# A four-layer graph network on one core: two chunks of the last layer by fetched neighbour lists, and two reorderings in the first layers

## The chip, the cores and the metric

The kernel runs on one core of a Trainium2 chip. The metric is the device time of one execution in microseconds (us). A profile of one execution shows what each engine did: TensorE (PE; its weight loads are PEld), VectorE (DVE), ScalarE (ACT), GpSimd (POOL), SyncE (SP), and the 16 DMA engines that move data.

## The reference

There are 2708 nodes with 512 features in `x`, and `adj` is a symmetric matrix of zeros and ones in which a node has about 16 neighbours. Four layers follow one another. Each adds its result to its input and normalizes every row.

```python
deg = jnp.maximum((adj != 0).astype(jnp.float32).sum(-1), 1.0)
x = _layernorm(x + _L0_gnn_ref(x, adj, deg[..., None], L0_gnn_W, L0_gnn_b), axis=-1)
x = _layernorm(x + _L1_gnn_ref(x, adj, L1_gnn_W, L1_gnn_b), axis=-1)
x = _layernorm(x + _L2_gnn_ref(x, adj, L2_gnn_W_stack), axis=-1)
x = _layernorm(x + _L3_gnn_ref(x, adj, L3_gnn_W, L3_gnn_b), axis=-1)
```

Layer 0 is `relu(((D (adj + I) D) x + x) W + b)` with `D = rsqrt(deg)`. Layer 1 is `(D' adj D' x) W^T + b`, where `D'` comes from the row sums of `adj`. Layer 2 is twice an attention: scores of every pair of nodes, a softmax over all nodes, multiplied by `adj`, and a weighted sum of the rows. Layer 3 is `adj (x W) + b`, with the eight heads side by side.

## The kernel before

**Tiling.** The nodes are 22 blocks of 128 (the last, block 21, has 20). `CH` cuts the result columns into six chunks: four of 512, then 384 and 276. `GROUPS` cuts the 22 blocks that are summed over into six groups: four of 4 blocks, then two of 3. Layers 0, 1 and 3 compute, for each chunk `k`, the transposed sum `acc[d] = sum over blocks j of x_j[:, d]^T adj[j, chunk]` in four banks (`d` is a quarter of the features). `multiply` does one group of one chunk. Each product is made twice, with the high part of the rows (`xh`) and the low part (`xl`), which `halve` makes in the first chunk. The factor from `adj` is a page `m`, which `prepare` casts on ScalarE from bytes (`at`) loaded by `load_bytes`; layer 0 casts from floats and writes the bytes (`masks`) for the layers after. `evict` copies `acc` to pages `ht`, `project` multiplies these by the weights (`mm`), and `combine` and `finish` add the residual (`xres`), normalize and store.

**Order.** Every engine runs its instructions in the order in which the program issues them (`Ordered`). `step` is one group: `before_products` loads two groups ahead and prepares one ahead, then come the products, then one phase of `ends` of the chunk before. Pages (82 of them, 128 by 512 floats) and banks come from pools: a new tile waits until the last use of the tile that had its place has ended, DMAs included.

**Layer 0.** The last group of a chunk is followed by `degree_ends`: products with ones count the neighbours (`deg`, `cnt`), VectorE makes `dg` of them, POOL multiplies four pages `xt` by `dg`, VectorE works out `dis` and `rdeg`, and then `evict` adds `xt` to `acc` as it writes `ht`.

**Layer 1.** `prepare` ends with `note`: VectorE takes maxima over the bytes in pieces of 32 nodes (`feeds`). From them `index` makes, later and between other work, the lists `givers`: for each block the numbers of the rows that are neighbours of its nodes. A full block has 4 lists of 128 rows that serve all its nodes and 8 that serve one quarter each; block 21 has 3.

**Layer 2.** `Attention` computes in the same chunks. `scores` fills pages `s`, `soften` takes the exponent, sums (`sum`), multiplies by the bytes and stores to `pairs` in HBM, beside three copies of the value rows (`pairs<-z_sb`). `fetch` gathers the rows of a list with an indirect DMA on POOL (`g`), into 11 wide buffers, and `weigh` makes `acc<-g`; lists of quarters go four side by side. A clock of planned costs (`advance`, `later`) decides where in the order of issue these stand. `normalize` ends a chunk of the second attention: the rows `r` are stored to `saved[2]` by SP (`x<-r`).

**Layer 3.** The first three chunks (`TWO = 3`) multiply their groups 0 to 3 while the attention ends (`early`). After that `step` goes through groups 4 and 5 of chunks 0 to 2 and all groups of chunks 3 to 5. Residual rows come through POOL's queue (`residual`).

Of the kernel before, what the change touches and what calls it, by code (L numbers as in the profile page):

```python
# [8 lines left out]
FP = mybir.dt.float32  # L9
# [10 lines left out]
P = 128  # L20
N = 2708
# [21 lines left out]
PAGES, WIDES = 82, 11  # L43
TWO = 3
LN_EPS = 1e-5
DEG_EPS = 1e-8
# [41 lines left out]
class Kernel:  # L88


    def __init__(self, ctx, tc, x_in, x_t, adj, adj_t, w0, b0, w1, b1, w2, w2_t, w3, b3, out):
# [33 lines left out]
            scratch.tile([P, D], FP, tag=f"y_{i}", name=f"y_{i}") for i in range(NB)  # L125
        ]

        self.masks = [
# [357 lines left out]


def cost(columns):

    return 4 * columns / 2400  # L490
# [25 lines left out]
class Fast:  # L516
# [4 lines left out]
    def __init__(self, kernel):  # L521
        self.k, self.tc = kernel, kernel.tc
        self.nc = Ordered(kernel.tc)

    def page(self, name, dtype=FP, shape=(P, BANK)):
# [8 lines left out]
    def run(self):  # L534
        kernel, nc = self.k, self.nc
        with ExitStack() as ctx:
# [10 lines left out]
            self.attention = attention = Attention(self)  # L547
            self.jobs, self.due, self.other, self.beats = [], None, 1, 0
            run = Run(l0, l1)
            for t in range(len(run.seq)):  # L550
# [11 lines left out]
            run.seq += [(l3, k, g) for k in range(2, TWO) for g in (4, 5)]  # L562
            run.seq += [(l3, k, g) for k in range(TWO, len(CH)) for g in range(len(GROUPS))]
            attention.run(self.early(run))
            for j in range(*GROUPS[5]):
                l3.rows[j] = attention.made[j]
            for t in range(4 * TWO, len(run.seq)):
                self.step(run, t)

            ly, k = run.before  # L570
# [236 lines left out]
    def prepare(self, ly, k, g, between=None, late=False):  # L807


        nc, (c0, cw) = self.nc, CH[k]  # L810
        ats = ly.done.pop(("at", k, g), None)
        if ats is None:
            return
        ms = []
        for j, at in zip(range(*GROUPS[g]), ats):
            if k == 0:
                self.halve(ly, j)
            m = self.page(f"m{ly.number}_{k}_{j}", FR)
            nc.scalar.copy(m[:, :cw], at[:, :cw])
            ms.append(m)  # L820
            if between:
                between()
                between = None
        ly.done["m", k, g] = ms
        if ly.number == 0:
            self.examining = self.examine(ly, k, g, ats)
            if k == 0 or g > 0:
                self.checked()
            else:
                next(self.examining)  # L830
        if ly.number == 1:
            at = ly.done.pop(("bytes", k, g))
            if late:
                return lambda: self.note(k, g, at)
            self.note(k, g, at)

    def note(self, k, g, at):
# [55 lines left out]
    def multiply(self, ly, k, g, only=None, ds=range(DC)):  # L893
# [9 lines left out]
        if blocks[-1] == NB - 1:  # L903


            blocks = blocks[:-1]
            for x in (ly.hi, ly.lo):
                for d in range(DC):
# [28 lines left out]
    def degree_ends(self, ly, k):  # L937
# [22 lines left out]
        for c in range(DC):  # L960
            nc.gpsimd.tensor_mul(xt[c][:, :cw], xt[c][:, :cw], dg[:, :cw])
        for _ in self.rsqrt(self.k.dis[:, i0 : i0 + n], cnt, DEG_EPS):
            pass
# [49 lines left out]
    def residual(self, ly, k):  # L1013
        for i, _, _ in blocks_of(k):
            t = self.page(f"xres{ly.number}_{i}")
            self.nc.gpsimd.dma_start(t, ly.source[i])
            ly.done["xres", i] = t
# [64 lines left out]
    def before_products(self, run, t):  # L1082
# [23 lines left out]
        if t + 1 < len(seq) and seq[t + 1][0].number == ly.number:  # L1106
            self.prepare(*seq[t + 1])
        if ly.number == 0 and g == len(GROUPS) - 2:
# [5 lines left out]
    def step(self, run, t):  # L1114
# [6 lines left out]
        if ly.number == 1 and k == len(CH) - 1 and g in (2, 3, 4):  # L1121
            self.attention.begin(g - 2)
        self.multiply(ly, k, g)
        if g == len(GROUPS) - 1 and k in ly.begun:
# [4 lines left out]
        if run.before:  # L1129
            self.ends(run, run.phase)  # L1130
            run.phase += 1
            if run.phase in ((3, 4, 5) if wide else (4,)):
                self.work("DVE")
        if g == (4 if ly.number == 3 and k < TWO else 3):
            self.residual(ly, k)
        if g == len(GROUPS) - 1:
            if ly.number == 3:
                self.biased(ly, k)
            if ly.number == 0:
                ends = self.degree_ends(ly, k)  # L1140
                next(ends)
                if k == len(CH) - 1:
                    note = self.prepare(
                        *run.seq[t + 1], between=lambda: next(ends), late=True
                    )
                for _ in ends:
                    pass
            while run.before and run.phase < 2:
                self.ends(run, run.phase)
                run.phase += 1  # L1150
            if k in ly.acc:
                self.evict(ly, k)
            if ly.number == 0:
                self.checked()
            run.before, run.phase = (ly, k), 0
# [212 lines left out]
class Attention:  # L1368
# [29 lines left out]
    def blank(self):  # L1398
# [3 lines left out]
        for pairs in (p for ly in self.pairs for p in ly):  # L1402
            self.nc.sync.dma_start(
                pairs[N:, : 2 * PAIR + D].rearrange("j (r d) -> j r d", d=D),
                t[:n, :].unsqueeze(1).to_broadcast([n, (2 * PAIR + D) // D, D]),
            )

    def begin(self, step):
# [370 lines left out]
    def normalize(self, ch):  # L1779
# [4 lines left out]
        def rest():  # L1784
            for _ in work:
                pass
            for (i, _, _), (r, _) in zip(ch.blocks, ch.ends):
                self.nc.sync.dma_start(self.k.saved[2][i], r)
                self.made[i] = r

# [113 lines left out]


@with_exitstack
def kernel(
# [61 lines left out]
```

## Time and profile before

| | us |
|---|---|
| median of 3 runs | 2306.28 |
| lowest, highest | 2305.75, 2307.77 |
| the profiled execution, whole | 2307.16 |
| its span, first to last instruction | 2305.3 |
| TensorE busy in the span | 2272.8 |
| VectorE, ScalarE, POOL busy | 1409.5, 675.9, 706.5 |
| bytes moved | 486.34 MB, 211 GB/s on average |
| mean granted TensorE clock | 0.995 |

A line of the profile's groups reads: line, engine, operation, output <- input, shapes, count; then busy time and the mean of one in ns; then the idle time of the engine just before, and what ended it. A line of the timeline reads: start, length, engine, line, operation, tiles, and in brackets the idle time before it with its releaser. Almost every line of code is L71 because a helper issues all instructions, so groups are told apart by their tiles. Products are pipelined, and their ends are modelled: the distance between two starts says more than a length. Of layer 3, chunk 3's projection begins at 2214.03 us and chunk 5's products end at about 2284.4.

### The profile page before, as it was taken

The page shows a single profiled execution, that of the slowest core. Times are in us where ns is not written, and L with a number is a line of the kernel's source. Part 1 is how long each engine was busy: PE and PEld are TensorE (multiplying, and loading weights), DVE is VectorE, ACT ScalarE, POOL GpSimd, SP SyncE. Part 2 cuts the span into 40 slices and gives each one's busy share as a digit, 9 for nine tenths or more (in the row PEclk, how much of TensorE's full clock was granted, in tenths as well). Part 3 has the DMA queues.
Part 4 walks back from the last instruction along what each step waited for, and adds up shares of the span by engine and source line. Part 5 has one row for each costly group of instructions (what it writes and reads, how often), then busy time and mean ns, then how long its engine had stood idle before and what let it go on. Part 6 is the DMA issues. An engine that isn't in the chain of part 4 may idle for free.

```text
span 2305.3 us, 25891 instructions
## 1 busy us (share of the span) xinstructions
PE 2272.8 (99%) x8525; PEld 1292.4 (56%) x8525; DVE 1409.5 (61%) x2803; ACT 675.9 (29%) x1354; POOL 706.5 (31%) x822
## 2 busy tenths in 40 slices
PE   9999999999999999999999999999999999899997
PEld 6676777778644444443555444444443455476685
DVE  6777886786554538748667511228769789625523
ACT  7444352323111123222332200113222334342211
POOL 3333431111000001635466550001635467542000
PEclk9999999999999999999999999999999999999999
DMA  9966762222556505868699998504868799973311
GB/s 347 288 189 179 188 182 76 76 82 77 194 191 263 182 5 181 296 205 300 236 331 336 337 411 320 185 5 165 301 228 288 250 324 332 338 219 120 117 51 43
DMA packets 260929, 486.34 MB, mean 211 GB/s; under 512 B 40238, under 2 KB 126950, under 8 KB 260784
## 3 DMA queue, kind: packets, MB, share of 16 engines
q1 hardware_dynamic: 192128, 269.63, 33.6%
q0 software_dynamic: 68656, 214.96, 28.0%
q8 instruction: 69, 1.13, 0.2%
q14 instruction: 76, 0.62, 0.1%
HBM read 307.55 MB, written 176.92 MB: 210 GB/s over the span
## 4 chain that ended last, share of the span: by engine, by line
PE 87%; DMA 5%; DVE 4%; issue 2%; ACT 1%; POOL 1%; SPq 0%; DVEq 0%; POOLq 0%; ACTq 0%
PE sp L71 33%; PE acc L71 30%; PE mm L71 8%; PE z L71 6%; PE wst L71 6%; DMA at<-in_adj_t 1%; DMA g<-pairs,givers 1%; PE mix L71 1%; DMA xr<-y 1%; PE list L71 1%; DMA mask<-some 1%; DMA x<-x 0%; PE tr_x2t L71 0%; PE tr_x2b L71 0%; DVE xl L71 0%
## 5 line engine op out<-in xcount | busy, mean ns | idle before, releaser
L71 PE MATMUL sp<-xs,wst_sb 128*128 128x512 f32 (+3 forms) x2112 | 798.3, 545 | 0.0
L71 POOL DMA_INDIRECT g<-pairs,givers x510 | 525.6, 1031 | 870.6 <-DMA xr<-x 242.3
L71 PEld LDWEIGHTS sp<-xs,wst_sb 128*128 128x128 f32 (+1 forms) x2112 | 380.5, 186 | 407.7 <-issue 325.6
L71 PE MATMUL acc<-m,xh 128*128 128x512 f32 (+4 forms) x1584 | 567.8, 380 | 7.4 <-ACT m L71 5.8
L71 PE MATMUL acc<-m,xl 128*128 128x512 f32 (+4 forms) x1584 | 551.0, 366 | 3.5 <-DVE xl L71 3.5
L71 PEld LDWEIGHTS acc<-m,xh 128*128 128x128 f32 (+1 forms) x1584 | 288.6, 188 | 72.0 <-issue 21.6
L71 PEld LDWEIGHTS acc<-m,xl 128*128 128x128 f32 (+1 forms) x1584 | 289.1, 189 | 48.0 <-issue 5.5
L71 PE MATMUL acc<-g 128*32 128x512 f32 (+1 forms) x1020 | 265.7, 609 | 2.9 <-DMA g<-pairs,givers 2.5
L71 ACT COPY s<-sp 128x512 f32<-128x512 f32 (+2 forms) x252 | 132.6, 528 | 396.3 <-PE sp L71 389.8
L71 ACT ACTIVATE s<-s 128x512 f32<-128x512 f32 (+3 forms) x264 | 151.7, 580 | 323.5 <-DVE s L71 323.2
L71 DVE TENSOR_TENSOR top<-top,s 128x512 f32<-128x512 f32 (+2 forms) x240 | 149.4, 623 | 155.6 <-ACT s L71 153.9
L71 PE MATMUL mm<-w,ht 128*128 128x512 f32 (+1 forms) x528 | 224.1, 594 | 3.4 <-DVE ht L71 3.4
L71 ACT CAST m<-at 128x512 fp32r<-128x512 uint8 (+5 forms) x396 | 199.6, 567 | 60.9 <-DMA at<-mask 20.2
L71 DVE TENSOR_TENSOR s<-s,shift 128x512 f32<-128x512 f32 (+3 forms) x264 | 162.9, 620 | 38.2 <-ACT shift L71 38.2
L71 DVE TENSOR_TENSOR s<-s,a 128x512 f32<-128x512 f32 (+3 forms) x264 | 165.9, 628 | 15.1 <-DMA a<-mask 6.0
L71 DVE TENSOR_TENSOR sum<-sum,s 128x512 f32<-128x512 f32 (+4 forms) x252 | 156.9, 623 | 13.9 <-ACT s L71 13.9
L71 PEld LDWEIGHTS mm<-w,ht 128*128 128x128 f32 (+1 forms) x528 | 95.9, 186 | 121.2 <-issue 111.4
L71 PEld LDWEIGHTS acc<-g 128*32 128x32 f32 (+1 forms) x1020 | 75.8, 135 | 146.1 <-issue 118.0
L71 PE MATMUL z<-w,xt 128*128 128x512 f32 (+1 forms) x352 | 151.0, 596 | 0.0
L71 PE MATMUL wst<-xt,mixed 128*128 128x512 f32 (+2 forms) x384 | 150.5, 545 | 0.0
L71 POOL DMA_DIRECT2D x<-o x44 | 26.0, 597 | 354.8 <-DVE o L71 350.6
L71 PEld LDWEIGHTS wst<-xt,mixed 128*128 128x128 f32 x384 | 72.1, 190 | 71.0 <-issue 59.0
(168 smaller groups left out, 1495.3 us busy)
## 6 DMA issues: line engine op xcount, KB each, us to landing
pairs<-z_sb SPq DMA_DIRECT2D x84, 768.0 KB
pairs<-s SPq DMA_DIRECT2D x168, 256.0 KB
at<-in_adj_t SPq DMA_DIRECT2D x84, 256.0 KB
xres<-x POOLq DMA_DIRECT2D x44, 256.0 KB, 4.9
x<-o POOLq DMA_DIRECT2D x43, 256.0 KB, 2.9
pairs<-s SPq DMA_DIRECT2D x84, 128.0 KB
x<-x SPq DMA_DIRECT2D x37, 256.0 KB
at<-mask SPq DMA_DIRECT2D x32, 256.0 KB
```

The lines of the kernel that those rows point to most:

```text
L71: ins = call(*args, **kw)
```

## The change

Two parts of layer 0 and 1, and one of layer 3 with what feeds it.

- **Layer 3.** The products run over chunks 0 to 3 only. Blocks 16 to 21 (chunks 4 and 5) are computed by a new class `Listed`: it gathers the rows of each list from a new tensor `sided`, sums them with products like those of the attention, turns the sum with four transposes, projects it and finishes it. A row of `sided` holds, for each pair of blocks, 128 columns of `adj`, the 512 features of the row, and 128 columns of `adj`. Its gathers begin after the attention; its products stand between those of chunk 3 from group 1 on, by a planned clock.
- **What feeds it.** `give` stores the cast pages `m` of layer 1's last two chunks to `sided` as floats (88 stores on SP). `normalize` stores each block of rows three times to `sided`, on SP, behind the store to `saved[2]` of the same block. `blank` writes zeros to the rows past the last node. `residual` of layer 3 uses SP's queue.
- **Layer 0.** In the last group of a chunk the products of `d` 0 and 1 come first, then the counting products, then `d` 2 and 3. `degree_ends` yields after POOL's products, and its last part comes behind `evict`.
- **Layer 1.** In chunk 0, `note` of groups 1 to 5 is put off: one is done in group 2, two each in groups 3 and 4, what is left at the end.

```diff
+DENSE = 4
+LISTED = CH[DENSE][0] // P
+SIDED = D + 2 * P
...
-            run.seq += [(l3, k, g) for k in range(TWO, len(CH)) for g in range(len(GROUPS))]
+            run.seq += [(l3, k, g) for k in range(TWO, DENSE) for g in range(len(GROUPS))]
...
+            self.listed = Listed(self, l3)
             for t in range(4 * TWO, len(run.seq)):
                 self.step(run, t)
+            self.listed.end_all()
...
+            if ly.number == 1 and k >= DENSE:
+                self.give(k, j, m)
...
+    def give(self, k, j, m):
+        n, lo, cw = rows_of(j), 0, CH[k][1]
+        while lo < cw:
+            i = (CH[k][0] + lo) // P - LISTED
+            w = min(P if i % 2 == 0 else 2 * P, cw - lo)
+            at = i // 2 * SIDED + i % 2 * (D + P)
+            self.nc.sync.dma_start(
+                self.k.sided[j * P : j * P + n, at : at + w], m.bitcast(FP)[:n, lo : lo + w]
+            )
+            lo += w
...
-            for x in (ly.hi, ly.lo):
+            for x in (ly.hi, ly.lo) if 0 in ds else ():
...
             nc.gpsimd.tensor_mul(xt[c][:, :cw], xt[c][:, :cw], dg[:, :cw])
+        yield True
...
-            self.nc.gpsimd.dma_start(t, ly.source[i])
+            (self.nc.sync if ly.number == 3 else self.nc.gpsimd).dma_start(t, ly.source[i])
...
-            self.prepare(*seq[t + 1])
+            late = ly.number == 1 and (k, g) < (0, len(GROUPS) - 1)
+            note = self.prepare(*seq[t + 1], late=late)
+            if late:
+                self.notes.append(note)
...
-        self.multiply(ly, k, g)
+        if self.listed and k == DENSE - 1 and g > 0:
+            for d in range(DC):
+                self.multiply(ly, k, g, ds=[d])
+                self.listed.beside(few_us(k, g) / DC)
+        elif ly.number == 0 and g == len(GROUPS) - 1:
+            self.multiply(ly, k, g, ds=range(2))
+            ends = self.degree_ends(ly, k)
+            next(ends)
+            self.multiply(ly, k, g, ds=range(2, DC))
+        else:
+            self.multiply(ly, k, g)
+            if self.listed:
+                self.listed.advance(few_us(k, g))
...
+        if ly.number == 1 and k == 0:
+            for _ in range(max(0, g - 1) if g < len(GROUPS) - 1 else len(self.notes)):
+                if self.notes:
+                    self.notes.pop(0)()
...
             if ly.number == 0:
-                ends = self.degree_ends(ly, k)
-                next(ends)
                 if k == len(CH) - 1:
...
-                for _ in ends:
-                    pass
+                else:
+                    next(ends)
+                next(ends)
...
             if ly.number == 0:
+                for _ in ends:
+                    pass
                 self.checked()
...
                 self.nc.sync.dma_start(self.k.saved[2][i], r)
+                rows = self.k.sided[i * P : (i + 1) * P, P:]
+                self.nc.sync.dma_start(
+                    bass.AP(
+                        rows.tensor,
+                        rows.offset,
+                        [rows.ap[0], (SIDED, (NB - LISTED) // 2), (1, D)],
+                    ),
+                    r.unsqueeze(1).to_broadcast([P, (NB - LISTED) // 2, D]),
+                )
...
+class Listed:
+    AHEAD = WIDES - 1
...
+    def beside(self, us):
+        self.advance(us)
+        end = self.clock + 1.6 * us
+        while self.clock < end and self.weigh():
+            pass
...
+    def weigh(self, wait=False):
+        nc, f = self.nc, self.f
+        if not self.to_weigh:
+            return False
+        i, n, ts, first, last = self.to_weigh[0]
+        there = self.fetched[len(ts) - 1][1]
+        if there > self.clock:
+            if not wait:
+                return False
+            self.advance(there - self.clock)
+        self.to_weigh.pop(0)
+        gs = [self.fetched.pop(0)[0] for _ in ts]
+        if first:
+            self.acc = f.bank(self.half, f"acc3_{i}")
+        odd, side = (i - LISTED) % 2, len(ts) > 1
+        for h, g in enumerate(gs):
+            lo, rows = (h * QW, QW) if side else (0, n)
+            e, z = (D + lo, 0) if odd else (0, P - lo)
+            nc.tensor.matmul(
+                self.acc[lo : lo + rows],
+                g[:, e : e + rows],
+                g[:, z : z + D],
+                start=first,
+                stop=last,
+            )
+        self.advance(1.1 if side else cost(D))
+        if last:
+            acc = self.acc
+            self.later(0, lambda: self.turn(i, n, acc))
+        self.fetch_ahead()
+        return True
...
+    def end_all(self):
+        while self.to_weigh or self.pending:
+            if not self.weigh(True):
+                self.advance(self.pending[0][0] - self.clock)
```

`Listed.fetch_ahead` keeps ten gathers ahead and plans 1.3 us for each and 6 us to land. `turn` copies the sum with VectorE, transposes it, copies it back with ScalarE and adds the bias to the residual rows; `project` makes `mm`; `end` adds, takes the statistics, and after every second block normalizes and stores.

## The prediction

> **What bounds the kernel now.** I read the page first, then the waits of TensorE, then the chain in order of time for layer 3, and then the stage in which layer 2 ends.
>
> ```profile
> PE 2272.8 (99%) x8525; PEld 1292.4 (56%) x8525; DVE 1409.5 (61%) x2803; ACT 675.9 (29%) x1354; POOL 706.5 (31%) x822
> PE 87%; DMA 5%; DVE 4%; issue 2%; ACT 1%; POOL 1%; SPq 0%; DVEq 0%; POOLq 0%; ACTq 0%
> ```
>
> TensorE is busy for 2272.8 of 2305.3 us and makes 87% of the chain that ended last: time is saved by taking work from TensorE or by closing its few gaps. The timeline of TensorE, with each gap and its releaser in brackets, shows those that the change can touch:
>
> ```profile
> 66.30 14.00 PE L71 MATMUL mm<-w,ht 128*128 128x512 f32 x32 [0.72 <-DVE ht L71]
> 227.10 13.14 PE L71 MATMUL mm<-w,ht 128*128 128x512 f32 x30 [1.25 <-DVE ht L71]
> 271.28 9.28 PE L71 MATMUL mm<-w,ht 128*128 128x512 f32 x21 [1.44 <-DVE ht L71]
> 331.57 0.49 PE L71 MATMUL acc<-m,xh 128*128 128x512 f32 x1 [1.07 <-ACT m L71]
> 333.60 0.79 PE L71 MATMUL acc<-m,xl 128*128 128x512 f32 x1 [1.53 <-DVE xl L71]
> 2004.71 0.50 PE L71 MATMUL acc<-m,xh 128*128 128x512 f32 x1 [3.42 <-ACT m L71]
> 2016.20 0.50 PE L71 MATMUL acc<-m,xh 128*128 128x512 f32 x1 [1.60 <-ACT begun L71]
> ```
>
> Three belong to layer 0 (ht), two to layer 1's first chunk, two to the end of layer 2. From 2016 us to the end of the products nothing holds TensorE. Layer 3's end in the chain (start, length, what):
>
> ```profile
> 2214.03 13.73 PE mm L71 x32
> 2227.76 28.38 PE acc L71 x176
> 2256.14 10.30 PE mm L71 x24
> 2266.44 18.06 PE acc L71 x143
> ```
>
> The acc pieces hold 144 of chunk 4's 176 products and all of chunk 5's; mm is a projection. The same chain around 1990:
>
> ```profile
> 1988.11 5.12 DMA x<-r
> ...
> 1993.32 0.56 DVE sum L71
> ...
> 2009.22 4.30 DMA pairs<-s
> ...
> 2016.20 44.96 PE acc L71 x200
> ```
>
> and the windows of 10 us there (length; busy PE, PEld, DVE, ACT, POOL; clock; DMA share; GB/s):
>
> ```profile
> 1980.00:1990.00 10.00, 9.95 (x28) 4.56 (x28) 7.19 (x17) 1.25 (x2) 7.83 (x8) 0.91 0.99 375
> 1990.00:2000.00 10.00, 10.00 (x45) 8.26 (x44) 7.85 (x20) 4.46 (x8) 2.86 (x3) 1.00 1.02 374
> ```
>
> Here TensorE is not the bound. Four rows r of attention chunk 3 are stored (x<-r, issued at 1987.17); VectorE's sum copy cannot start until the store has landed, since its page is one that r held; it heads the softening of chunk 5, whose last stores gate ScalarE's casts and so TensorE at 2016.20. And the DMA engines are full: share 1.0, 374 GB/s.
>
> **What the Trainium skill says.** "DMA: Bandwidth & Descriptors", section "Issuing engines are not separate DMA queues": DMAs of all issuing engines run on the same 16 DMA engines and interleave. The trace agrees: the 1 MB of x<-r takes 6.1 us to land (1987.2 to 1993.3) beside POOL's gathers. Its section "Queues, rings and completion order": each engine takes turns between the queues that have work, packet by packet; so SP's stores and POOL's gathers should share the bandwidth about equally. No row shows the turns themselves. "TensorE: Matmul & The Clock Gate", section "What's actually happening": after an idle window of about 3.4 us TensorE runs at half clock until busy again for as long. The trace has it after less: the gaps at 331 and 333 us are followed by six products 0.43 us apart instead of 0.227.
>
> **Layer 3, removed.** Chunk 4 and 5's products: 28.38 + 18.06 from the chain, and chunk 4's first group, which lies in the piece before, 32 x 0.173 (spacing of the 384-wide products in the timeline) = 5.5: 52.0 us. Their projections: 10.30 + 8.7 (2284.4 to 2293.1) = 19.0.
>
> **Layer 3, added.** Five full blocks, each 4 lists alone and 2 rounds of 4 quarters side by side, and block 21 with 3 lists. A list is the attention's acc<-g product: 3.43 us for four in the chain's pieces, so 0.858; a round of quarters takes 1.06 in the timeline. 23 x 0.858 + 10 x 1.06 = 30.3. Each block's sum is turned by four transposes (tr_top: 0.49 to 0.60 us): 6 x 0.5 = 3.0. Projections 5 x 3.43 + 1.0 = 18.2. Sum of removed and added: -71.0 + 51.5 = -19.5 us on TensorE.
>
> **Are the lists there in time?** There are 63 gathers, each 0.95 us on POOL plus 0.30 between them (the POOL timeline: 1.26 us pitch), landing 4.0 to 4.8 us after issue where DMA is calm. Ten go out at once behind the end of attention; some 77 us of layer 3's other products cover them. The other 53 start as buffers come free in chunk 3: 53 x 1.26 = 67 us, against 75 us of TensorE work there as I add it up in the order of the clock that Listed keeps. POOL is not continuous, for only ten are in flight: following the order with these prices, the last gather goes out about 152 us after group 4 of chunk 0 begins (2099), and TensorE wants it at 155; it lands at 156 to 157. So 1.6 us of wait, then about 1.0 for the last block's copy on VectorE before its transposes and 0.9 for ScalarE's before its projection: nothing is ordered between them. With half a microsecond of colder clock: +4. Ends: +2 if gathers land in 3.5, +10 if their pitch is 1.5. In (3, 1) VectorE has chunk 2's combine and finish (about 7 us) ahead of block 16's copy: some 2 us of wait, which the gathers would otherwise have cost, so not added. After the last projection the tail (12.1 us from the last mm to the end) has the same operations: chunk 3's last block instead of chunk 5's. Layer 3: -15.5.
>
> xres loads go from POOL to SP. Ahead of at<-mask on SP stands out<-o today, till 2135.8, and POOL's xres of those steps went out by 2132; nothing is later. 0.
>
> **Layer 0 and 1.** The count's products go ahead of half of the last group, so POOL's four xt products (5.06 us) and ht come 1 to 1.8 us sooner, and rsqrt's steps go behind ht. The three gaps sum to 3.4; I take 2.5 (0 to 3.4; a both not yet ready could cost 1 of it). In layer 1 two feeds maxima of 2.2 us leave VectorE's queue ahead of the late xl: 4.4 against gaps of 2.6, plus 1.3 of half clock; I take 3 (1 to 3.9). Later they fill idle VectorE time (it is 64% to 87% busy there). Sum -5.5. The 88 small stores of layer 1's casts (give) are about 0.37 us each on SP (the median of pairs<-z_sb): 8 per group, 3 us in steps of 4 to 5.5 us, and the byte loads behind them are two groups ahead; DMA is at 0.23. 0, or +2 if a cast waits. Four stores of zeros near 73 us: 0, at most +1 at the existing gap of 97 us.
>
> **The moved traffic: 22 stores of rows into sided.** Each writes a row block three times, as pairs<-z_sb does: 768 KB. They stand in SP's queue between the x<-r of a chunk, 3.1 MB for four blocks, 17 MB in all. Where chunk 3 ends (1987) the engines are full, r's pages now come free only when these too have landed, and the chain runs through that. SP then has 4.2 MB; about 2.9 MB of gathers share with it (six more issued, about three outstanding): 7.1 MB at 400 GB/s is 17.7 us, and about 1 to land: 2006 instead of 1993.3. That is 12; which page sum gets is not certain (the third r would be 2 us sooner), so 11, all of it on TensorE, which stands from 2001 on. Behind the stores in SP's queue are the row loads x<-x and softening's pairs<-s; those are wanted later than sum's page. Bounds: 0 to 14; nothing there is made faster. The bursts at 1700 and 1799 delay a<-mask by 8 us or so, while the first masked product comes 24 us after the load (1703 to 1727); at 1896 the s pages come back later, with four banks of 2 us to cover; at 2055 and 2101 DMA is at 0.5 to 0.8 and one cast already waits 2.1 us for x<-r with 3.8 us in hand. For all of these +2 (0 to 12).
>
> **Sum.** -15.5 - 5.5 + 11 + 2 = -8. The profiled execution took 2307.16 around its span of 2305.3 and is 0.9 above the median 2306.28; from the median, 2298.3, and I write 2299.
>
> **Rivals.** (1) The burst stays hidden: the page that sum waits for is another, or the stores land ahead of the gathers. For it: many pages, a choice I cannot see. Against it: sum, a cast and an xl all wait for x<-r there. -15.5 - 5.5 + 2: 2287. (2) Slower: the stores hold up softening at every chunk's end, at 1700, 1799 and 1896, through pages of s or masks that come back 8 to 12 us late, ScalarE's copies stop, and TensorE's score banks fill. Against: bank cover, and no ScalarE wait of this kind now beyond 1.5 us. It decides from 12.6 us in sum, about 4 us for each end; with 6 each, 18 in the place of the 2 counted, it is 2314. (3) The gathers set layer 3's end: pitch 1.5 instead of 1.26 puts TensorE 8 us later: 2306, no change. Against: gaps in DMA there (0.2 to 0.3).
>
> **Numbers.** 0.2% of the median is 4.6 us, about what a measurement of this kernel tells from nothing. The likeliest case 0.50 (own range 2292 to 2306), rival (1) 0.25, (2) 0.14, (3) 0.11. Faster: 0.43 of the first and all of (1), 0.68; same: 0.06 of the first, most of (3) and a little of (2), 0.18; slower 0.14. Range: 2286 to 2309.
>
> **What the changed profile would show.** Right: no acc products of 384 or 276 columns in layer 3, gathers into sided's lists at 1.26 us, a copy and two gaps of about 1 us before the last projection; the ht gaps of layer 0 and the xl gap at 333 gone; and, near 2000, a TensorE gap of some 15 us behind ScalarE's casts, with a DMA of sided in the chain in the place of x<-r. Wrong: that gap as it was (rival 1), or new waits of sp products in 1700 to 1930 (rival 2), or acc<-g waits summing to over 8 us after 2180 (rival 3).

## The result: 0.5% slower

The changed kernel takes 2318.85 us (median of 6 runs, 2315.47 to 2319.65), the kernel before 2306.02 beside it: a ratio of 1.005 with a 95% interval of 1.0038 to 1.0061, 12.8 us slower. The prediction said 2299 and at most 2309. The profiled execution took 2319.55 us around a span of 2317.8.

TensorE does have less to do, as the page after says (busy time of each engine, then the chain by engine):

```profile
PE 2260.6 (98%) x8323; PEld 1254.4 (54%) x8323; DVE 1395.0 (60%) x2812; ACT 659.7 (28%) x1313; POOL 757.0 (33%) x863
PE 87%; DMA 6%; DVE 4%; ACT 2%; issue 1%; SPq 1%; POOL 0%; ACTq 0%; DVEq 0%; POOLq 0%
```

It is busy 12.2 us less in a span 12.5 us longer, so it stands still some 25 us longer (products at a slow clock count as busy). To see where, I set the same TensorE instructions of both traces beside each other (start in us; `begun` are pages in which ScalarE keeps the sums that layer 3's early products have begun):

| instruction | before | after | after minus before | lost since the row above |
|---|---|---|---|---|
| first turn of layer 1's rows (tr_x2t) | 388.0 | 387.8 | -0.2 | -0.2 |
| first wst (layer 1 is over) | 604.8 | 614.4 | +9.7 | +9.8 |
| last sp (last scores of layer 2) | 1948.0 | 1958.6 | +10.7 | +1.0 |
| acc restart behind begun (layer 3 runs freely) | 2016.2 | 2033.3 | +17.1 | +6.5 |
| last mm (last projection) | 2292.5 | 2300.8 | +8.2 | -8.9 |
| end of span | 2305.3 | 2317.8 | +12.5 | +4.3 |

Only one stretch is clearly faster, layer 3, and by less than said. The timeline of TensorE after, with the gaps that answer to those shown of before:

```profile
97.26 0.50 PE L76 MATMUL acc<-m,xh 128*128 128x512 f32 x1 [3.26 <-ACT m L76]
100.02 0.80 PE L76 MATMUL acc<-m,xh 128*128 128x512 f32 x1 [2.02 <-ACT m L76]
609.68 0.60 PE L76 MATMUL acc<-m,xh 32*128 32x276 f32 x4 [8.06 <-ACT m L76]
2021.84 0.79 PE L76 MATMUL acc<-m,xh 128*128 128x512 f32 x1 [5.68 <-ACT m L76]
2033.33 0.50 PE L76 MATMUL acc<-m,xh 128*128 128x512 f32 x1 [1.48 <-ACT begun L76]
2280.27 1.11 PE L76 MATMUL tr<-ident,sum 128*128 128x128 f32 x4 [4.05 <-DVE sum L76]
2282.06 5.55 PE L76 MATMUL mm<-w,turned 128*128 128x512 f32 x8 [0.68 <-ACT turned L76]
```

The three ht gaps of layer 0 and the two of layer 1 at 331 and 333 us are gone, as the reorderings intended. But the gap near 97 us, 1.0 before, is now 5.3 in two pieces; one of 8.1 has come at 609 us, where nothing stood before; and two stand at the very end. Three of these are ScalarE's casts being late; the last is VectorE's queue. The chain after, at layer 3's end:

```profile
2270.94 3.45 PE mm L76 x8
2274.41 0.70 DVE xres L76
...
2276.04 2.38 DVE xres L76 x4
2278.43 1.20 DVE ht L76 x2
2280.27 1.13 PE tr L76 x4
2282.06 15.87 PE mm L76 x32
```

Between the last list and its transposes VectorE first ends block 19 (it waits for its mm until 2274.41), then adds the biases of chunk 3's four blocks and copies two ht. All of that was put into its queue ahead of the copy of the last list's sum.

At 609 us one must go two engines back. The timeline of SP's queue after:

```profile
589.65 3.75 SPq L76 DMA_DIRECT2D sided<-m  x8
...
600.62 0.40 SPq L76 DMA_DIRECT2D at<-mask  x1
```

and of ScalarE:

```profile
608.56 1.07 ACT L76 CAST m<-at 128x276 fp32r<-128x276 uint8 x3 [12.48 <-DMA at<-mask]
```

The eight stores of give could not go out before 589.65, since the casts they read stood on ScalarE behind a copy (sums<-list) that waited for TensorE until 589.03. Behind them in SP's queue stand eight weight loads and then the last load of mask bytes; in the kernel before, SP issued that load 18 us earlier:

```profile
582.76 0.32 SPq L71 DMA_DIRECT2D at<-mask  x1
```

It went out late, and the last casts with it.

Finally, each gap costs more than its length, for TensorE runs at half clock for a while. The clock granted in 90 to 100 and 100 to 110 us is 0.89 and 0.76, in 600 to 620 us 0.82 and 0.83, in 2270 to 2290 us 0.95 and 0.71: each time this is a stretch of 6.8 us at half clock. But part of each stretch lies in the gap itself, where nothing is lost by it. Half of the time that TensorE was busy in the stretch is the loss: 2.4, 1.8 and 2.4 us. At 609 us, 8.1 and 1.8 make the 9.8 of the table. The kernel before lost 1.5 at such a place (0.83 in 330 to 340).

### The profile page after: what moved, and what is told of

It is laid out like the page before. It is cut to its first block, busy times and chain, and to the rows that moved or that the text cites. A ratio compares the mean times of both kernels' runs of the same rounds, so it can differ in the third digit from the quotient of the medians.

```text
span 2317.8 us, 25756 instructions
## 1 busy us (share of the span) xinstructions
PE 2260.6 (98%) x8323; PEld 1254.4 (54%) x8323; DVE 1395.0 (60%) x2812; ACT 659.7 (28%) x1313; POOL 757.0 (33%) x863
## 3 DMA queue, kind: packets, MB, share of 16 engines
q0 software_dynamic: 71936, 228.69, 29.3%
## 4 chain that ended last, share of the span: by engine, by line
PE 87%; DMA 6%; DVE 4%; ACT 2%; issue 1%; SPq 1%; POOL 0%; ACTq 0%; DVEq 0%; POOLq 0%
PE sp L76 33%; PE acc L76 29%; PE mm L76 9%; PE z L76 6%; PE wst L76 6%; DMA x<-x 2%; DMA at<-in_adj_t 2%; DMA pairs<-s 1%; ACT m L76 1%; SPq L76 1%; PE mix L76 1%; DMA g<-pairs,givers 1%; DVE xres L76 1%; DVE xl L76 1%; PE list L76 1%
## 5 line engine op out<-in xcount | busy, mean ns | idle before, releaser
L76 PE MATMUL acc<-m,xh 128*128 128x512 f32 (+3 forms) x1408 | 522.8, 392 | 21.2 <-ACT m L76 19.7
L76 PE MATMUL acc<-m,xl 128*128 128x512 f32 (+3 forms) x1408 | 501.9, 373 | 1.7 <-DVE xl L76 1.7
L76 PEld LDWEIGHTS acc<-m,xh 128*128 128x128 f32 (+1 forms) x1408 | 257.9, 189 | 90.2 <-issue 25.7
L76 PE MATMUL acc<-g 128*32 128x512 f32 (+2 forms) x1146 | 298.6, 607 | 6.6 <-DMA g<-pairs,givers 5.3
L76 PEld LDWEIGHTS acc<-m,xl 128*128 128x128 f32 (+1 forms) x1408 | 258.2, 190 | 47.9 <-issue 6.9
L76 ACT CAST m<-at 128x512 fp32r<-128x512 uint8 (+5 forms) x352 | 182.6, 579 | 84.0 <-DMA at<-mask 29.3
L76 PE MATMUL mm<-w,ht 128*128 128x512 f32 (+1 forms) x480 | 205.1, 593 | 0.0
L76 PEld LDWEIGHTS acc<-g 128*32 128x32 f32 (+2 forms) x1146 | 84.6, 135 | 165.9 <-issue 132.6
L76 PEld LDWEIGHTS mm<-w,ht 128*128 128x128 f32 (+1 forms) x480 | 88.2, 187 | 107.8 <-issue 103.7
```

Source lines behind the costliest of these rows:

```text
L76: ins = call(*args, **kw)
```

## Experiments

**Theory after the result**: the loss is made in several places, by the added stores and the order in which instructions stand in SP's, ScalarE's and VectorE's queues, not by the lists' work. **Rivals**: one place, the burst at layer 2's end, makes it; the reorderings are worth nothing; the lists cost what they save.

Beside the first and the last group of four the kernel before takes 2323 to 2325 us, beside the others 2307 to 2308, for a reason that is not known (the second and the last group have the same chip number); so ratios are compared, and times only within a group.

### The reorderings alone

The kernel before, with the two hunks of the diff on count and notes and nothing else.

> The kernel before with the two reorderings alone (layer 0's count ahead of half of the last group, layer 1's feeds maxima put off); no lists, no sided. Theory, several places: the reorderings are sound and the loss lies in the added stores, so this is 4 to 6 us faster than before: 2300 to 2302 us, with the ht gaps of layer 0 (0.7, 1.3 and 1.4 us) and the gaps at 331 and 333 us gone. Rival, the reorderings give nothing (in the changed kernel the time at the start of layer 1's transposes was the same as before): 2305 to 2307 us.

Measured: 0.9979 (0.9964 to 0.9994), 4.9 us faster. The named gaps are gone, but one of 4.6 us, with half a microsecond behind it, stands near 98 us, although this kernel stores no zeros into sided. So in this execution something else made casts late. A candidate is in the timeline of ScalarE, here in the changed kernel:

```profile
67.42 0.20 ACT L76 ACTIVATE rs_t<-rs_v 128x4 f32<-128x4 f32 x1 [5.71 <-DVE rs_v L76]
```

rsqrt's first step (rs_v, VectorE) now stands behind the four ht sums, which wait one by one for POOL's products. ScalarE, in order, stands 5.7 us at the square root, where it stood 1.2 before, and all casts are behind it. That this wait makes the gap is not shown: the next run has the same wait (5.72 us at 66.21) and no gap there.

### Mends of one cost each

**Zeros into sided stored in layer 1's second chunk**, not layer 0's, where they stand ahead of the loads of `adj_t` in SP's queue (that queue before, then after):

```profile
69.46 7.04 SPq L71 DMA_DIRECT2D pairs<-blank  x4
76.62 29.13 SPq L71 DMA_DIRECT2D at<-in_adj_t  x23
```

```profile
74.21 5.59 SPq L76 DMA_DIRECT2D pairs<-blank  x4
79.84 10.03 SPq L76 DMA_DIRECT2D sided<-blank  x4
89.99 15.91 SPq L76 DMA_DIRECT2D at<-in_adj_t  x19
```

```diff
         if ly.number == 0 and (k, g) == (1, 0):
             self.attention.blank()
+        if ly.number == 1 and (k, g) == (1, 3):
+            self.attention.blank_sided()
```

> The changed kernel with the stores of zeros into sided moved from layer 0's second chunk to layer 1's second chunk. Theory: the zeros stand ahead of the loads of adj_t in SP's queue for some 10 us and cost the gaps at 97 and 100 us and a stretch at half clock, 5 to 7 us in all: 2312 to 2314 us, against 2318.8 for the changed kernel, and the 97 us gap back at about 1 us. Rival, the zeros are hidden (the loads were late before, too) and what layer 0 lost lies in its reordering: 2318 to 2320 us.

Measured: 1.0037 (1.0021 to 1.0052). No gap near 97 us in its trace, and tr_x2t starts at 379.5 rather than 387.8. In the time it is 3 us, with intervals that overlap. Up to there the kernel issues what e1_order_only does, whose trace starts tr_x2t at 389.2: one trace of each can't tell small effects in this stretch.

**Casts stored behind the next load of bytes**: prepare only notes them, and they go out a step later.

```diff
-                self.give(k, j, m)
+                self.given.append((k, j, m))
...
         if t + 2 < len(seq):
             self.load(*seq[t + 2])
+        for one in self.given:
+            self.give(*one)
+        self.given = []
```

> The changed kernel with the stores of layer 1's casts into sided (give) issued one step later, behind the next load of mask bytes instead of ahead of it. Theory: the stores wait in SP's queue for casts and hold the load that the next casts need, which costs the 8 us gap at 609 us and its half clock, 9 to 10 us: 2308 to 2310 us, and no gap above 2 us there. Rival, the volume of the stores is the cause and not their place (the load is as late behind full DMA engines): 2317 to 2320 us.

Measured: 1.0016 (1.0000 to 1.0032), 7.8 us less than the changed kernel's 1.005. SP's queue here:

```profile
579.04 3.79 SPq L76 DMA_DIRECT2D sided<-m  x8
...
586.75 0.49 SPq L76 DMA_DIRECT2D at<-mask  x1
591.45 3.90 SPq L76 DMA_DIRECT2D sided<-m  x8
```

The stores still wait for their casts until 591.45, but the load is ahead of them. No TensorE gap is left there, and tr_x2t to wst takes 216.9 us (before 216.7, changed 226.6). The bytes are the same: it was the place in the queue.

**Chunk 3's rows copied from saved[2] later**, so that r's pages come free early:

```diff
-                rows = self.k.sided[i * P : (i + 1) * P, P:]
-                self.nc.sync.dma_start(
...
                 self.made[i] = r
+                if ch.k != 3:
+                    self.side(i, r)
+            if ch.k == 3:
+                for n, (i, _, _) in enumerate(ch.blocks):
+                    self.later(28 + 3 * n, lambda i=i: self.side(i, self.k.saved[2][i]))
```

> The changed kernel with chunk 3's four stores of rows into sided taken out of the burst at layer 2's end: they are copied from saved[2], in DRAM, 28 us and more later by the attention's clock, so that the pages of r come free when saved[2] is stored, as in the kernel before. Theory: of the loss between 1950 and 2034 us (6.5 us in the two traces) 5 to 7 come back: 2312 to 2314 us, and a gap behind ScalarE's casts of about 3.4 us, as before, in the place of 5.7. Rival, the pages are not what is waited for and the same bytes delay others wherever they stand: 2317 to 2320 us.

Measured: 1.0044 (1.0029 to 1.0060), 1.4 us: not to be told from the changed kernel. The gap behind the casts is only 0.3 in its trace, so it looked half right. It is taken up again below.

### The square root, the zeros of the pairs, the end, and all together

The kernel of e1_order_only, with the first two steps of rsqrt back ahead of the ht sums:

```diff
-        yield True
-        for _ in self.rsqrt(self.k.dis[:, i0 : i0 + n], cnt, DEG_EPS):
-            pass
+        root = self.rsqrt(self.k.dis[:, i0 : i0 + n], cnt, DEG_EPS)
+        next(root)
+        yield True
+        for _ in root:
+            pass
```

> The kernel before with the two reorderings, and with rsqrt's first two steps (rs_v on VectorE, the square root on ScalarE) left ahead of the ht sums, where they are in the kernel before. Theory: in the reordering as made, rs_v stands behind the four ht sums, these wait for POOL's products, and ScalarE stands in order at its square root for 5.7 us with the casts behind it, at each of layer 0's chunk ends; so this is 2 to 4 us faster than the reorderings alone (ratio 0.9979): 0.996 to 0.997, the ScalarE wait at 61 to 67 us is under 2 us, and pairs<-blank starts near 70 us again rather than 74. Rival, the casts have cover and nothing follows from that wait: 0.998.

Measured: 0.9957 (0.9944 to 0.9970), 9 us faster than before; against e1_order_only's 0.9979 the intervals just overlap. ScalarE's row and SP's:

```profile
60.70 0.20 ACT L71 ACTIVATE rs_t<-rs_v 128x4 f32<-128x4 f32 x1 [1.19 <-DVE rs_v L71]
```

```profile
69.75 5.93 SPq L71 DMA_DIRECT2D pairs<-blank  x4
75.79 30.05 SPq L71 DMA_DIRECT2D at<-in_adj_t  x26
```

The wait is 1.2, the zeros go out at 69.75 (74.2 in the changed kernel), the gap near 97 us is closed, and tr_x2t starts at 378.6, 9.4 us before the kernel before.

The next moves the pairs' zeros as well (blank called in layer 1's second chunk):

> The kernel of e9_sqrt_ahead with the stores of zeros into the pairs (3.5 MB, four stores, in the kernel before too) moved from layer 0's second chunk to layer 1's second chunk. Theory: SP's queue and the DMA engines set the gap near 97 us, and any zeros there cost; this takes the rest of it: 1 to 4 us more, ratio 0.994 to 0.9965, no gap near 97 us. Rival: the gap comes from the wide buffers, not from the zeros: same ratio as e9_sqrt_ahead.

Measured: 0.9991 (0.9985 to 0.9998): worse by 0.3%. SP issues pairs<-blank for 8.2 us from 383.1, the mask load behind it is at 391.5, and TensorE stands:

```profile
404.05 0.80 PE L71 MATMUL acc<-m,xh 128*128 128x512 f32 x1 [2.62 <-ACT m L71]
```

Again stores stand ahead of a load in SP's queue, as with give. Here nothing holds them but their own 8.2 us of issue.

The end alone: ht copies ahead of the work beside the last group, biases a group earlier, chunk 3's projections ahead of the last list's:

```diff
                 self.multiply(ly, k, g, ds=[d])
+                if g == len(GROUPS) - 1 and d == DC - 1:
+                    self.evict(ly, k)
                 self.listed.beside(few_us(k, g) / DC)
...
+        if self.listed and k == DENSE - 1 and g == 4:
+            self.biased(ly, k)
...
-            self.listed.end_all()
+            while self.listed.to_weigh:
+                self.listed.weigh(True)
             ly, k = run.before
-            parts = self.project(ly, k)
+            parts = self.project(ly, k, between=lambda: self.listed.advance(DC * cost(D)))
+            self.listed.end_all()
```

> The changed kernel with its end alone reordered: chunk 3's ht copies ahead of the work beside its last group, its biases one group earlier, and its projections ahead of the last list's transposes and projection. Theory: at the end VectorE's queue (the end of block 19, four biases, two ht copies) stands ahead of the copy of the last list's sum and costs the gaps of 4.1 and 0.7 us and a stretch at half clock: 5 to 6 us, ratio 1.0025 against 1.005, no TensorE gap over 1 us after 2260 us. Rival, the last lists are late whatever the order: 1.0045 to 1.0055.

Measured: 1.0021 (1.0012 to 1.0030), 6.7 us less than 1.005. From the acc restart to the last mm takes 260.1 us, where the changed kernel takes 267.4 and the kernel before 276.4; no gap after 2220. The end behind the last mm has grown from 17.0 to 18.5, since VectorE's sums of chunk 3 now queue behind the last list's.

All of these, with both kinds of zeros in layer 1 (the misplaced ones too):

> The changed kernel with every mend: rsqrt's head ahead of the ht sums, all zeros stored in layer 1's second chunk, layer 1's casts stored behind the next load of bytes, chunk 3's rows copied into sided 28 us and more later, and at the end chunk 3's ht copies and biases ahead of the last lists' work on VectorE and its projections ahead of the last list's. Theory, several places: each mend gives back what it cost (9.5 for the casts, 6 for the rows, 5 to 8 in layer 0, 5 to 6 at the end of layer 3), so about 26 of 2318.8 us: ratio 0.991 to 0.995, faster than the kernel before. Rival, the lists' own work (gathers, more DMA, the longer end of POOL) costs what they save: ratio 0.997 to 1.0, no faster than the kernel of e10_zeros_too.

Measured: 0.9971 (0.9962 to 0.9980). Faster than before, but not by as much as expected: the ratio lies in the rival's range. Its trace has the misplaced zeros' gap of 4.1 us at 405.8, and 18.5 us behind the last mm.

### The mended kernel, and what the lists are worth

Pairs' zeros back in layer 0, sided's in layer 1; each sum of chunk 3 combined right behind its projection; and the flag of the last branch worked out before chunk 3's projections:

```diff
+            self.flag()
+            (ly, k), made = run.before, []
+            def between(i, n, ps):
+                if len(made) < len(blocks_of(k)) - 1:
+                    made.append((i, n, self.combine(ly, k, len(made), i, n, ps)))
+                self.listed.advance(DC * cost(D))
+            parts = self.project(ly, k, between)
+            self.listed.end_all()
```

> The changed kernel with the mends that the runs so far bear out: rsqrt's head ahead of the ht sums; the pairs' zeros where they were and only sided's four zero stores in layer 1's second chunk; layer 1's casts stored behind the next load of bytes; chunk 3's rows copied into sided later; at the end ht copies and biases early, each of chunk 3's sums combined right behind its projection, and the flag (bad_ps) worked out ahead of chunk 3's projections, so that POOL's last drain starts early. Theory: against e11_all (ratio 0.9971) the gap of 4.1 us at 405 us and its half clock go (5.5 us) and 6 to 9 us between the last projection and the end: 0.9905 to 0.993. Rival, the end is bound by POOL's drain after the gathers: 0.994 to 0.995.

> The kernel of e9_sqrt_ahead (the two reorderings with rsqrt's head ahead of the ht sums, no lists) with the flag worked out ahead of the last projections, as in e12_mended. Theory: 0 to 1.5 us off e9_sqrt_ahead's 0.9957: 0.995 to 0.996; e12_mended against this one is what the lists are worth when their stores are out of the way: 6 to 12 us. Rival, the lists gain nothing even then: e12_mended at the same ratio as this.

> e12_mended with chunk 3's four stores of rows into sided back in the burst, from the pages of r, as in the changed kernel. Theory: the pages come free late, VectorE and with it ScalarE's casts stand, and this is 3 to 7 us slower than e12_mended (0.0015 to 0.003 in the ratio), with a gap behind the casts near 2007 us of 5 us or more in the place of about 3.3. Rival, the burst costs nothing in the end: within 1 us of e12_mended.

Measured: e12_mended 0.9930 (0.9915 to 0.9945; 2292.97 us against 2307.92), e13_no_lists 0.9956 (0.9942 to 0.9970; 2298.70), e14_rows_in_burst 0.9932 (0.9917 to 0.9946; 2292.09). The mended kernel beats both kernels. It lies at the edge of what was expected, and the lists are worth 5.7 us of it, a little under the 6 to 12 expected; each of its six runs is faster than each of the five without lists. Its end on TensorE:

```profile
2257.27 1.92 PE L76 MATMUL acc<-g 128*32 128x512 f32 x16
...
2259.57 7.11 PE L76 MATMUL mm<-w,ht 128*128 128x512 f32 x16
2266.52 0.60 PE L76 MATMUL tr<-ident,sum 128*128 128x128 f32 x4
```

The projections of ht cover the last sum's copy and turn; nothing waits. And the third kernel, with chunk 3's rows back in the burst, is as fast. There its stores are in the chain:

```profile
1982.42 6.24 DMA sided<-r
...
1991.43 9.53 DMA x<-x
```

In e12_mended x<-r takes that place (5.17 us), but gathers are late ahead of it (gaps of 3.6 and 0.7 us behind them), and its stretch from last sp to restart is 75.5 us against 73.2. Another wait of the same size stands there.

The square root alone, in the changed kernel:

> The changed kernel with rsqrt's first two steps ahead of the ht sums and nothing else. Theory: the square root that stands in ScalarE's queue for 5.7 us at each of layer 0's chunk ends is the largest cost in layer 0; with sided's zeros still ahead of the loads of adj_t some gap near 97 us stays: 5 to 9 us faster than the changed kernel, ratio 1.001 to 1.003, and layer 1's transposes start 5 to 9 us before their 387.8 us. Rival, sided's zeros alone keep the gap near 97 us whole: ratio 1.004 to 1.0055.

Measured: 1.0037 (1.0024 to 1.0051), 3 us, with intervals that overlap; 5 to 9 were expected. tr_x2t at 385.0, 2.8 before the changed kernel's; with sided's zeros still in layer 0, four gaps of 2.5 us in sum remain near 97. Against e9_sqrt_ahead, which has no zeros of sided, 6.4 us are left, put down to the zeros. All traces of reordered kernels together bear the zeros out: tr_x2t starts at 385.0 to 389.6 in the five with sided's zeros in layer 0, and at 378.3 to 381.8 in the twelve without, but for two (386.3 in e18_rows_after, 389.2 in e1_order_only). The square root's 2.8 they don't: the four traces with zeros and the root unmended, which issue the same up to there, lie between 386.4 and 389.6.

### The rows of layer 2's end once more

Only the stores of r into sided, which nothing reads, in the kernel without lists; all 22, and those of chunks 0 to 2; and, with lists, all copied during layer 3's first chunks.

```diff
                 self.nc.sync.dma_start(self.k.saved[2][i], r)
+                rows = self.k.sided[i * P : (i + 1) * P, P:]
+                self.nc.sync.dma_start(
...
+                    r.unsqueeze(1).to_broadcast([P, (NB - LISTED) // 2, D]),
+                )
                 self.made[i] = r
```

> The kernel of e13_no_lists once more, beside the next three: 0.995 to 0.9965, and 68 to 72 us from the last sp product to the acc restart.

> e13_no_lists with nothing added but the 22 stores of rows r into sided (17 MB), which nothing reads. Traffic theory: 3 to 6 us slower than e13_again (0.0013 to 0.0026 in the ratio), and 72 us or more from the last sp product to the acc restart. Rival, the stretch varies by itself and the bytes are hidden: within 1.5 us of e13_again. The prediction's term was 11 + 2 = 13 us.

> e16_rows_only with the stores of chunks 3, 4 and 5 left out, so only the 12 stores of chunks 0 to 2. If the burst at chunk 3's end is what costs: as fast as e13_again. If the earlier chunks' bytes cost: as slow as e16_rows_only.

> e12_mended with all 22 rows copied from saved[2] into sided one at a time during layer 3's first chunks, none in the attention's stores. Traffic theory: layer 2's end goes back to 68 to 71 us and this is 3 to 5 us faster than e12_mended (0.993): 0.991 to 0.992. Rival, the copies collide with chunk 4's and 5's gathers and mask loads there: 0.993 or slower.

Measured: 0.9966 (0.9950 to 0.9981), 0.9983 (0.9970 to 0.9996), 0.9967 (0.9951 to 0.9982) and 0.9960 (0.9943 to 0.9978). From last sp to restart: 80.3, 80.3, 78.8 and 78.0 us. The stretch is as long without sided's rows as with them in this group; in the two groups before, and in the first pair of traces, it was 67 to 72 without and 73 to 76 with. In the time, all 22 stores are 4.1 us slower than none by the medians (-0.5 to 7.6 by resampling the runs), and those of chunks 0 to 2 make no difference (0.6). So in this kernel the stores cost something between nothing and 7 us, likeliest about 4; 13 us, as in the prediction, are excluded.

e18_rows_after missed: 0.9960 where 0.991 to 0.992 was expected, and beside e13_again the lists gain nothing (2.3 us slower by the medians, -4.9 to 5.1). Its trace has a new gap of 3.4 us behind casts at 2124.45, among the copies, and one of 2.5 us at 2248.48 for which the profile names no cause; the latter is also in the three traces with lists of the first group, and in none of the groups between. So what the lists are worth isn't settled beyond the group in which 5.7 us were measured.

One cut of all traces says more of the burst: from the first x<-r of chunk 3 to the restart. The kernel before takes 29.0 us (from 1987.17), the changed one 31.6 (from 2001.73); so 3.9 of the 6.5 us were lost ahead of the burst. The eleven traces without chunk 3's stores in the burst take 27.6 to 31.4 us (median 29.3), the seven with them 29.5 to 33.9 (31.6). The changed kernel's chain there:

```profile
2008.92 0.82 SPq L76
...
2011.35 9.85 DMA x<-x
...
2022.23 0.60 ACT m L76
```

It holds no store into sided and no wait for a page of r, but SP's time to issue the last of the eight stores, the row loads behind them, and a cast behind these.

## Why the prediction was wrong

By its own steps.

**"Added: ... -19.5" and "+4" of waits at layer 3's end.** The products were priced well: with the end mended, layer 3 takes 15.9 to 16.3 us less than before, 1.7 of waiting included, so the products gave about -18 of the -19.5. The failed term is the +4 of waits: up to the last mm the changed kernel gained only 8.9. "Nothing is ordered between them" was the error: VectorE had block 19's end, four biases and two ht copies in its queue ahead of the copy, so 7.3 us more than the mended order. The "half a microsecond of colder clock" was 2.4.

**"In (3, 1) ... some 2 us of wait."** Measured 1.7 (the gap at 2218.39 behind sum). Right. The gathers were in time: no acc<-g wait after 2180. Rival (3) falls.

**"After the last projection the tail has the same operations."** 17.0 instead of 12.7 us from last mm to end. The flag of the last branch, at 2303.03, is only 0.3 us later behind the last mm than before, and POOL's closing steps begin after it. From flag to end it is 14.8 us, 10.8 before: POOL's last drain takes 7.66 us in the profiles with gathers in layer 3, and 4.32 in those without, and the step ahead of it (INC_SWDGE_SEM) 2.06 instead of 1.24. With the flag earlier the tail is 13.9. Why the drain grows wasn't tried.

**"The count's products ... 2.5" and layer 1's 3.** Too low: with the square root kept ahead the two reorderings gain 9.4 us up to 388. TensorE's gaps there fall from 7.0 to 0.6 us, 1.5 of half clock go, and some 1.5 are not traced. But "rsqrt's steps go behind ht" was noted and not priced: it names no engine behind it, and ScalarE's casts were. 2.8 us in the changed kernel by one pair of traces, less than such traces differ by.

**"Four stores of zeros near 73 us: 0, at most +1."** Some 6. On SP they took 10.0 us to issue, the loads of adj_t behind them went out at 90.0 instead of 76.6.

**"The 88 small stores ... 0, or +2 if a cast waits."** +9.8 at one place, and 9.7 of it went when only the stores' place in the queue was changed (e4_give_behind). I took the stores' own 0.37 us each (they are 0.42 in the median) and "two groups ahead"; I didn't ask what the first of them waits for. In chunk 5's last groups that is a cast behind a copy behind TensorE.

**"The moved traffic": +11 and +2.** The largest term, priced at about twice what was measured or more. VectorE's xl did wait 4.3 us for sided<-r, but from the first x<-r on the changed kernel took 2.6 us more, not 11; with what came ahead of the burst it is 6.5 in one pair of traces, of which the times show about 4, and not beyond doubt. The path was wrong too: the row loads behind the stores, "wanted later than sum's page", are what the chain goes through. I added the bytes to one chain as if its other waits, gathers and row loads, stayed as they were; in e12_mended and e14_rows_in_burst, when one went, another of about the same length stood there.

So the sum of the stretches: 9.4 gained by the reorderings, 2.8 + 6.4 lost to the root and the zeros, +9.8, +1.0, +6.5, -8.9, +4.3: 12.5 us. The mends (6.4 + 2.8 in layer 0, 9.7 for give, 7 at the end, 3 in the tail) come to 28.9; the mended kernel's ratio is lower than the changed one's by 27.7 us. Several parts rest on single traces, so it is partly luck that the sums meet so well.

Between the -8 predicted and the +12.5 of the two spans lie 20.5 us: 10.9 in layer 3's waits and its tail, 9.8 in give's stores, 5.3 in layer 0 and the start of layer 1, and -5.5 in layer 2, where the burst had been priced too high. So the sum failed at what it put at nothing, the stores' places in SP's queue, and at the waits of layer 3's end; the burst's price hid part of it.

Of the rivals, (1) was nearest on the burst, and (2) ended on the right side by a mechanism that didn't happen: no sp product waited between 1700 and 1930. None had SP's queue at layer 0 and 1, where some 16 us were lost.

## What to carry to other kernels

In this kernel a store that waited for its data held every load behind it on the same queue, one of them for 18 us. Before placing one, name the instruction it waits for, what that waits for in turn, and the next load behind; put loads whose time is fixed ahead of stores whose time is not. The same holds for compute engines: an instruction moved "behind" another takes along whoever reads it first on a third engine. When a long wait is removed from a stretch in which several transfers end close together, count on the next of them, not on the whole gain. And a time at half clock is a loss only where the engine is busy in it.

## What the hardware showed that I had not expected

In the clock records of all 18 traces TensorE's half clock comes in pieces of 3.413 us: up to the end of the products each stretch lasts one, two or three of them, and within a trace all begin a whole number of pieces apart (those at 333.13 and 1954.46 us of the kernel before 475). What counted was how long TensorE stood still within one piece of this grid, not the length of a gap. Of the pieces at full clock (from 30 us to 25 us before the end), all 61 with 1.86 us or more of standstill were followed by half clock, 5 of 27 with 1.6 to 1.86, and 3 of 214 with 0.4 to 1.6. So two gaps of 1.1 and 1.5 us with one product between them brought half clock at 333 us (2.1 us in one piece), and one of 1.6 us at 2016 us did not (1.3 in one piece).

"TensorE: Matmul & The Clock Gate" of the Trainium skill, section "What's actually happening", has half clock after at least one idle window of about 3.4 us. The length of the pieces agrees with that. An idle window in the strict sense was not needed: 1.86 us of standstill in one piece were enough every time.

Four stores of zeros to 108 rows each, 0.29 MB in all, took 2.05 to 3.15 us each on SP behind 3.5 MB of others; the same four took 0.31 to 0.39 us in e12_mended, at 384 us, with no such stores ahead of them. And POOL's last drain took 7.66 us in all ten traces with 63 more gathers in the program, and 4.32 in the eight without.
